# A four-stage convolution network on one core: order of the tap stages' work, of the first bias products, of the layer changes, and another form of the gates

## The chip, the cores and the metric

The kernel runs on one core of a Trainium2 chip. The metric is the time of one launch in microseconds of the device, the median over several runs. The engines are called PE (TensorE: matrix products), DVE (VectorE), ACT (ScalarE), POOL (GpSimd) and SP (SyncE, which only issues transfers here). Transfers are issued from the queues of SP, ACT and POOL.

## The reference

Input x has 4 images of 256 channels and 56 x 56 points, in float32. Four layers follow, each as x = x + F(groupnorm(x)), with groups of 8 channels:

```python
# layer 0: involution: a 7x7 kernel for each point and each of 16 groups
h = einsum('bchw,oc->bohw', x, reduce_w) + reduce_b          # 64 channels
kern = einsum('bchw,oc->bohw', h, span_w) + span_b           # 16 * 49 taps for each point
out = (kern.reshape(b, G, 1, K*K, Ho, Wo) * patches).sum(axis=3)
# layer 1: two 3x3 convolutions, each with batch norm; relu(x + h)
# layer 2: involution as layer 0, with batch norm and relu after the reduce and after the sum
# layer 3: gates from Fourier transforms
cf = sigmoid(fft2(x).real.mean((-2, -1)) @ W.T + b)          # one value for each channel
sf = fft2(x.mean(1, keepdims=True)).real.mean(1)             # one value for each point
out = x * cf[:, :, None, None] + x * sf[:, None]
```

## The kernel before

All layers run in one program: `involution_layer(0)`, `conv_layer`, `involution_layer(2)`; the gates of layer 3 run inside layer 2, one image later. Channels lie on the 128 partitions, in two blocks (cb), and a block of an image is a tile of 128 x 3136 (`new_block`, three buffers). Each engine's instructions stand in the order in which the program writes them (`in_order`), so a step's place in the text is its place in its engine's queue. An engine waits only for what its next instruction needs, so a queue may run ahead of the others.

An involution works by units: image b, block cb, eight units. For each image `bottleneck` first makes h, the reduced input, as the tile `hp`: products of `redn` (the reduce weights times the norm's scale) and x into PSUM, then evictions with the bias `hb`. For layer 0's first image `begin` does this, in an order written out by hand. Each unit then has two stages:

- Tap stage, `tap_matrices`: 32 steps n, each with six products (L580) into a pair of PSUM banks, and an eviction into `kt` with the bias `zb_sb`, by ACT in six instructions (L591) for every third n and by DVE in one (L598) for the others. There are four such pairs of banks, for everything in these layers. `hooks` is a dictionary of other steps which are put in after the eviction of step n: the group norm's six steps for the block before (`norm_steps`: aggregate, product, small sums, product, power on POOL, shift), the channel mean, the gate factors, loads.
- Column stage, `apply`: seven columns tx of eight points. For each, 56 products of `kt` and a window matrix `xw` (L622), a sum on ACT and DVE, and then `next_windows` and `next_strip`. A strip is the normed input of one column with its border (`strip_sb`, one buffer), transposed by seven products (L396), copied to `xw` by ACT (L408), and shifted within `xw` by four transfers (L414, L416). There are three buffers of `xw`, so windows are three columns ahead. `early` and `late` hold steps put in before and after a column.

`zb_sb` comes from `window_biases`: 24 small products (L255) and one copy. In layer 0 it stands in `begin` ahead of the first norm; for layer 2 it is made at the beginning of the convolutions and goes through DRAM (`zb2_dram`).

`conv_layer` computes each 3 x 3 convolution with transformed columns: `row_weights` makes the transformed weights u1 to u4 (L1218 to L1225), `phases` spreads the normed input into four phases on ACT (L1290), `transform` makes the six tiles v on DVE (L1298 to L1320), then follow products (L1411, L1382, L1493). A list `after` gives the steps put in after each group of products.

In layer 2, `channel_mean` and `gate_factors` make cf and sf of the image before; sf goes through DRAM and comes back to all partitions. Its weights `w3` are loaded by SP into a part of the image's own block that is no longer used (`dead`). `gate_chunk` is one of 14 gates of an image, with 8 rows of a block each: load of x (`gx`, three buffers), four operations on POOL, and a store. `next_load` and `next_gate` take the load and the rest of the next one. With xn = rstd * x + shift, it computes x * (1 + cf * rstd) + cf * shift + xn * sf. The last image is done by `last_gates` and its companions in another form.

Of the kernel before, what the change touches and what calls it, by code (L numbers as in the profile page):

```python
# [16 lines left out]
P = 128  # L17
# [54 lines left out]
def net_kernel(  # L72
# [59 lines left out]
    for i in range(2):  # L132
        nc.scalar.dma_start(rp[i * R : (i + 1) * R, :], rpar)
    mhalf = const.tile([P, NB], F32, name="mhalf")
# [89 lines left out]

    def mark():
        return len(nc.cur_bb.bb.instructions)
# [23 lines left out]
    def window_biases(zb_sb, bias, ps):  # L250

        bias_f = bias[:G, KK * KK : KK * KK + ZN]
        for p in range(TP):
# [7 lines left out]
            )  # L261
        nc.scalar.copy(
# [17 lines left out]
    def involution_layer(layer, xin, xout, red, span, sb, xs_of, ahead=None, pending=None):  # L280

        with ExitStack() as es:
# [12 lines left out]
            def warm(n, by):  # L295

                ps = one_bank()
                for _ in range(n):
                    nc.tensor.matmul(ps[:, :P], ident_sb, by, start=True, stop=True)
# [6 lines left out]
            if layer == 0:  # L306
# [3 lines left out]
                nc.scalar.copy(norm_sb[:, 3, B - 1, 1, :], mhalf)  # L310

            red_sb = wpool.tile([P, NB, 2, R], F32, name="red_sb")

            def load_red():
                for i in range(2):
                    eng = nc.gpsimd if layer == 0 else nc.scalar
                    eng.dma_start(red_sb[:, :, i], red.rearrange("(cb p) r -> p cb r", p=P))

            if layer == 2:
                load_red()  # L320
# [41 lines left out]
            def next_strip():  # L362
# [15 lines left out]
                if layer == 2:  # L378
# [42 lines left out]
            def bottleneck(b):  # L421
# [4 lines left out]
                rstd, shift = norms[layer][b]  # L426

                redn = work.tile([P, NB, 2, R], F32, name="redn", bufs=1)
                for ci in range(NB):
                    nc.vector.tensor_scalar_mul(redn[:, ci], red_sb[:, ci], rstd[:, ci : ci + 1])  # L430
# [55 lines left out]
            def begin():  # L486
# [4 lines left out]
                biases = bias_table(scratch[:, n:], sb, nc.gpsimd.dma_start, nc.scalar.copy)  # L491
# [3 lines left out]
                load_red()  # L495
# [6 lines left out]
                window_biases(zb_sb, scratch[:, n:], one_bank())  # L502
                folds = batch_norms()
                sums0, sums1 = sums(0, 0), sums(0, 1)
                redn = work.tile([P, NB, 2, R], F32, name="redn", bufs=1)
                rstd, shift = norms[0][0]
                steps(sums0, NCHUNK)
                norm = norm_of(0, 0, 0, sums_of[0, 0])
                steps(norm, 2)
                warm(4, ident_sb)  # L510
                steps(norm, 2)
                warm(8, ident_sb)
# [7 lines left out]


                pairs = [two_banks() for _ in range(4)]
                bank = pairs[3][:, 1, :]
# [34 lines left out]
                for j in range(NH):  # L558
                    products(j, 1)
                for j in range(NH):  # L560
# [3 lines left out]
                    for py in range(min(rows, TY)):  # L564
                        dst = hp[:, py, :, a0 : a0 + n, :]
                        nc.scalar.activation(dst, s[:, py, :, :n, :], AF.Identity, bias=hb)
                return folds
# [1154 lines left out]
```

## Time and profile before

The median of three runs is 1817.9 us (1817.29 to 1822.03). One more execution was recorded by the profiler: 1812.46 us, of which 1810.7 are the span from the first to the last instruction. All times below are places in that span.

| what | from the profile |
|---|---|
| profiled execution, its span | 1812.46 us, 1810.7 us |
| mean granted clock of PE | 0.979 |
| tap products L580 | 392.1 us busy, 6144 passes |
| column products L622 | 379.0 us busy, 12544 passes |
| convolution products L1493, L1411, L1382 | 385.0, 212.3 and 98.6 us busy |
| tap evictions on DVE, L598 | 336, 319.8 us busy |
| tap evictions on ACT, L591 | 1056 instructions, 306.9 us busy |
| gate operations on POOL | L789 and L794 31.7 us each, L795 49.0, L796 48.7, 42 of each |
| layer 0, convolutions, layer 2 | up to about 507 us, to 1243 us, to the end |

How to read it: a product in float32 shows as two passes. PE's busy time counts matmuls whose ends are modelled, so a busy PE is not one at its peak. The granted clock is 1.00 at full speed, and in places of low activity it is 0.50. The time of an idle engine costs nothing unless the engine is the one that all others wait for.

### The profile page before, as it was taken

What the parts mean: (1) busy time and instruction counts of PE and PEld (TensorE: products, weight loads), DVE (VectorE), ACT (ScalarE), POOL (GpSimd) and SP (SyncE); (2) the same over time, 40 slices, a digit from 0 to 9 for tenths busy, and PEclk for the clock granted to TensorE, in tenths of its full rate; (3) what the DMA queues carried; (4) which work ended last, traced back from release to release, by engine and by line L of the source; (5) the groups of instructions that cost most, each with busy time, mean ns of one, the idle gap of its engine ahead of it and who ended that gap; (6) DMA issues with size and microseconds to landing.
All of it is one profiled execution on the core that took longest, in us unless ns stands there. A gap on an engine that the chain in (4) does not pass through costs nothing.

```text
span 1810.7 us, 55835 instructions
## 1 busy us (share of the span) xinstructions
PE 1720.8 (95%) x24034; PEld 1514.9 (84%) x24034; DVE 1375.4 (76%) x2729; ACT 842.2 (47%) x1981; POOL 430.0 (24%) x626
## 2 busy tenths in 40 slices
PE   7999999999989999999999999997999999899988
PEld 6998989889878988998899889985988887887876
DVE  3787777776689988898889888875777677677775
ACT  3566556555532322322232222113767567577564
POOL 2333433245210000000000000000000374563572
PEclk9999999999989999999999999998999999999997
DMA  2545534454651201120121111031534566665653
GB/s 85 158 154 165 164 119 143 159 159 116 209 174 49 69 26 63 63 70 30 59 73 59 41 60 34 34 135 49 161 132 149 168 218 188 202 210 168 169 156 127
DMA packets 66004, 215.77 MB, mean 119 GB/s; under 512 B 13237, under 2 KB 20926, under 8 KB 62046
## 3 DMA queue, kind: packets, MB, share of 16 engines
q1 hardware_dynamic: 48718, 145.24, 25.7%
q0 software_dynamic: 14688, 64.78, 11.3%
q8 instruction: 190, 3.11, 0.7%
q10 hardware_dynamic: 2352, 2.18, 0.4%
q14 instruction: 56, 0.46, 0.1%
HBM read 76.30 MB, written 49.15 MB: 69 GB/s over the span
## 4 chain that ended last, share of the span: by engine, by line
PE 76%; DVE 9%; ACT 6%; DMA 4%; issue 2%; POOL 2%; SPq 1%; ACTq 0%; POOLq 0%; DVEq 0%
PE mm L1493 19%; PE ps L580 18%; PE ps L622 14%; PE mm L1411 10%; PE mm L1382 5%; PE ps L396 5%; DMA xw<-xw 4%; ACT kt L591 3%; PE ps L459 2%; DVE un L642 1%; DVE kt L598 1%; ACT xw L408 1%; ACT hp L478 1%; SPq L414 1%; DVE res L1486 1%
## 5 line engine op out<-in xcount | busy, mean ns | idle before, releaser
L580 PE MATMUL ps<-hp,z_sb 64*126 64x133 f32 x6144 | 392.1, 281 | 16.2 <-ACT kt L591 7.0
L622 PE MATMUL ps<-kt,xw 126*32 126x48 f32 (+1 forms) x12544 | 379.0, 236 | 24.1 <-DMA xw<-xw 12.1
L622 PEld LDWEIGHTS ps<-kt,xw 126*32 126x32 f32 (+1 forms) x12544 | 341.9, 122 | 68.2 <-issue 46.3
L580 PEld LDWEIGHTS ps<-hp,z_sb 64*126 64x126 f32 x6144 | 369.1, 187 | 34.6 <-ACT kt L591 12.7
L598 DVE TENSOR_TENSOR kt<-ps,zb_sb 126x798 f32<-126x798 f32 x336 | 319.8, 981 | 90.1 <-PE ps L580 89.5
L1493 PE MATMUL mm<-v,u_sb 128*128 128x280 f32 (+1 forms) x1728 | 385.0, 385 | 3.4 <-DVE v L1318 3.4
L1493 PEld LDWEIGHTS mm<-v,u_sb 128*128 128x128 f32 x1728 | 327.9, 190 | 57.5 <-DVE v L1318 3.8
L591 ACT ACTIVATE kt<-ps,zb_sb 126x133 f32<-126x133 f32 x1056 | 306.9, 442 | 96.2 <-PE ps L580 95.6
L1411 PE MATMUL mm<-v,u_sb 128*128 128x252 f32 (+1 forms) x936 | 212.3, 388 | 3.4 <-DVE v L1302 3.4
L1411 PEld LDWEIGHTS mm<-v,u_sb 128*128 128x128 f32 x936 | 178.3, 192 | 33.8 <-issue 3.5
L1530 POOL DMA_DIRECT2D x<-xs x24 | 13.1, 546 | 683.2 <-DVE xs L1529 427.4
L642 DVE SCALAR_TENSOR_TENSOR un<-ps,s,un 128x240 f32<-128x240 f32 x224 | 102.5, 457 | 85.7 <-ACT un L637 81.5
L642 DVE SCALAR_TENSOR_TENSOR un<-ps,par_sb,un 128x240 f32<-128x240 f32 x224 | 98.3, 457 | 87.1 <-ACT un L635 82.8
L1478 ACT ACTIVATE res<-xs,shift,norm_sb 128x1120 f32<-128x1120 f32 (+1 forms) x24 | 30.2, 1259 | 236.3 <-DVE xs L1529 107.3
L408 ACT COPY xw<-ps 126x896 f32<-126x896 f32 x112 | 101.4, 906 | 47.9 <-PE ps L396 37.7
L647 POOL TENSOR_TENSOR xs<-un,xs 128x240 f32<-128x240 f32 x112 | 72.3, 664 | 192.4 <-DVE un L642 192.3
L396 PE MATMUL ps<-ident_sb,strip_sb 128*126 128x128 f32 x784 | 111.7, 283 | 6.1 <-POOL strip_sb L381 5.8
L635 ACT ACTIVATE un<-ps,par_sb 128x240 f32<-128x240 f32 x112 | 50.1, 448 | 115.7 <-PE ps L622 113.4
L1382 PE MATMUL mm<-xs,u_sb 128*128 128x126 f32 (+1 forms) x792 | 98.6, 277 | 1.3 <-DVE xs L1345 0.9
L396 PEld LDWEIGHTS ps<-ident_sb,strip_sb 128*126 128x126 f32 x784 | 84.9, 142 | 17.0 <-POOL strip_sb L381 6.9
L637 ACT ACTIVATE un<-ps,bn_t,s 128x240 f32<-128x240 f32 x112 | 60.0, 538 | 83.3 <-PE ps L622 72.1
L1382 PEld LDWEIGHTS mm<-xs,u_sb 128*128 128x128 f32 x792 | 94.5, 191 | 2.4 <-issue 1.0
(254 smaller groups left out, 1925.8 us busy)
## 6 DMA issues: line engine op xcount, KB each, us to landing
xw<-xw SPq DMA_DIRECT2D x168, 252.0 KB
xw<-xw SPq DMA_DIRECT2D x224, 126.0 KB
xw<-xw POOLq DMA_DIRECT2D x56, 252.0 KB, 4.7
xs<-x SPq DMA_DIRECT2D x24, 560.0 KB
x<-xs POOLq DMA_DIRECT2D x8, 1568.0 KB, 8.2
xs<-x SPq DMA_DIRECT2D x8, 1568.0 KB
xs<-in_x_dram SPq DMA_DIRECT2D x6, 1568.0 KB
x<-xs SPq DMA_DIRECT2D x6, 1568.0 KB
```

The source lines that it names most:

```text
L396: nc.tensor.transpose(ps[:Q, k * P : (k + 1) * P], flat[:, k * Q : (k + 1) * Q], ident_sb)
L408: nc.scalar.copy(xw[:, :NSB, :], ps[:Q, : NSB * P].rearrange("q (n c) -> q n c", n=NSB))
L580: nc.tensor.matmul(ps[:Q, i, k * NT : (k + 1) * NT], z_sb[i * R : (i + 1) * R, cb * GB // 2 + gp, z0 : z0 + Q], hp[i * R : (i + 1) * R, py ...
L591: nc.scalar.activation(kt[:, g0 + i, pb, :, k], ps[:Q, i, k * NT : (k + 1) * NT], AF.Identity, bias=zb_sb[:, cb * GB + g0 + i, p0 + k : p0 ...
L598: nc.vector.tensor_tensor(kt[:, g0 : g0 + 2, pb], ps[:Q, :, : PB * NT].rearrange("q i (k t) -> q i t k", k=PB), zb_sb[:, cb * GB + g0 : cb ...
L622: nc.tensor.matmul(v[m * j : m * j + m, i, :, k * TP : (k + 1) * TP], xw[:, window(ty), m * j : m * j + m], kt[:, ng * j : ng * j + ng, :, ...
L637: nc.scalar.activation(part, o[0], AF.Identity, bias=bn["t4"][:, cb : cb + 1], scale=bn["s4"][ng][:, 0, cb : cb + 1])
L642: nc.vector.scalar_tensor_tensor(part, o[e], s, part, ALU.mult, ALU.add)
L647: nc.gpsimd.tensor_tensor(dst, u, dst, ALU.add)
L1382: nc.tensor.matmul(ps[:, co * m : (co + 1) * m], u[ci][:, co * P : (co + 1) * P], v2[:, e, : n // 2, ci * WT : (ci + 1) * WT], start=(ci = ...
L1411: nc.tensor.matmul(ps, u1_sb[:, ci, dy, k, co * P : (co + 1) * P], v[:, k, dy * NB + ci : (dy + n - 1) * NB + ci + 1 : NB, :], start=(j == 0),
L1493: nc.tensor.matmul(ps, u2_sb[:, ci, dy, k, co * P : (co + 1) * P], v[:, k, dy * NB + ci : (dy + n - 1) * NB + ci + 1 : NB, :], start=(j == 0),
```

## The change

- `red_sb`, the reduce weights, becomes one constant tile for both involutions; `redn` becomes a constant too. Layer 2's weights are loaded in `begin_conv` (near the end of layer 0) by SP instead of at layer 2's beginning by ACT's queue, and `redn` of its first image is made in `begin_last`, by `norm_weights`, in the last but one convolution.
- In `begin` the bias's load goes from POOL's queue to ACT's. Of the 24 bias products 14 stay ahead of the first norm and 10 go behind the reduce products; the copy follows the evictions into `hp`. The PSUM pairs are taken earlier, and the first norms and the warming products use one of them.
- An activation at the beginning is a Sigmoid instead of a copy (its result is overwritten later).
- Tap stages: ACT evicts n = 2, 5, ... 29 (10) instead of 0, 3, ... 30 (11).
- Layer 2's start: the first two strips are made by POOL; the first strip stands ahead of `bottleneck(0)`, and two windows stand ahead of the tap products instead of between them.
- In units 1 and 2 of layer 2 the steps of the norm stand at other n. `gate_factors` begins at n = 8 instead of 17, and w3 is loaded into the buffers of `sfb` (all images but the last).
- Gates: xn * (sf + cf + 1/rstd) - shift/rstd. Loads of sf are steps of their own, two ahead, and loads and gates stand at other places.
- Convolutions: in `row_weights` the third operation of both blocks follows the first two of both; at the beginning three products of 448 columns follow the bias products, and the weights' third operations follow the third step of `transform`.

```diff
+    red_sb = const.tile([P, NB, 2, R], F32, name="red_sb")
+    def load_red(red, eng):
+        for i in range(2):
+            eng.dma_start(red_sb[:, :, i], red.rearrange("(cb p) r -> p cb r", p=P))
+    def norm_weights(layer, b):
+        redn = redn_of[layer, b] = new_redn()
+        for ci in range(NB):
+            nc.vector.tensor_scalar_mul(redn[:, ci], red_sb[:, ci], norms[layer][b][0][:, ci : ci + 1])
...
-                nc.scalar.copy(norm_sb[:, 3, B - 1, 1, :], mhalf)
+                nc.scalar.activation(norm_sb[:, 3, B - 1, 1, :], mhalf, AF.Sigmoid)
...
-                if layer == 2:
+                if layer == 2 and len(strips) > 2:
                     nc.scalar.activation(dst, img, AF.Identity, bias=shift, scale=rstd)
                 else:
                     nc.gpsimd.tensor_scalar(dst, img, rstd, shift, ALU.mult, ALU.add)
...
-                biases = bias_table(scratch[:, n:], sb, nc.gpsimd.dma_start, nc.scalar.copy)
+                biases = bias_table(scratch[:, n:], sb, nc.scalar.dma_start, nc.scalar.copy)
...
-                window_biases(zb_sb, scratch[:, n:], one_bank())
+                pairs = [two_banks() for _ in range(4)]
+                bank = pairs[3][:, 1, :]
+                biases = window_biases(zb_sb, scratch[:, n:], bank[:, R:])
+                steps(biases, 14)
...
                 for j in range(NH):
                     products(j, 1)
+                steps(biases, TP - 14)
...
                         nc.scalar.activation(dst, s[:, py, :, :n, :], AF.Identity, bias=hb)
+                run(biases)
                 return folds
...
-                    if n % 3 == 0:
+                    if n % 3 == 2:
...
-                w3_sb = [dead(b, 1, 4 * CR * W + ci * C, C) for ci in range(NB)]
+                w3_sb = [new_sf()[:, :C] if b < B - 1 else dead(b, 1, 4 * CR * W + ci * C, C) for ci in range(NB)]
...
-                nc.vector.tensor_mul(scale, cf, norms[3][b][0])
-                nc.vector.tensor_scalar_add(scale, scale, 1.0)
-                nc.vector.tensor_mul(bias, cf, norms[3][b][1])
+                nc.vector.reciprocal(back, rstd)
+                nc.vector.tensor_add(cfx, cf, back)
+                nc.vector.scalar_tensor_tensor(back, shift, -1.0, back, ALU.mult, ALU.mult)
...
+            def load_sf(b, j):
+                sf_of[b, j] = new_sf()
+                nc.gpsimd.dma_start(sf_of[b, j], sf_dram[b][j : j + 1].to_broadcast([P, CR * W]))
...
-                nc.gpsimd.tensor_scalar(xs, xs, scale, bias, ALU.mult, ALU.add)
-                nc.gpsimd.tensor_tensor(xn, xn, sf, ALU.mult)
-                nc.gpsimd.tensor_tensor(xs, xs, xn, ALU.add)
+                nc.gpsimd.tensor_scalar(xs, sf_of[b, j], 1.0, cfx, ALU.mult, ALU.add)
+                nc.gpsimd.tensor_tensor(xs, xs, xn, ALU.mult)
+                nc.gpsimd.tensor_scalar(xs, xs, 1.0, back, ALU.mult, ALU.add)
+                if cb == 1 and j + 2 < NCHUNK:
+                    load_sf(b, j + 2)
...
+                next_strip()
                 run(bottleneck(0))
                 hooks0[3] = list(pending[0])
-            next_strip()
-            for i in range(NXW):
-                hooks0.setdefault(2 + 5 * i, []).extend((next_windows, next_strip))
+                for _ in range(NXW - 1):
+                    next_windows()
+                    next_strip()
+                hooks0[7] = [next_windows, next_strip]
...
-                        place(hooks, g, (19, 20, 22, 23, 25, 26))
+                        place(hooks, g, (15, 19, 20, 24, 25, 26))
...
-                            place(hooks, gate_factors(pb), (17, 24, 27, 28, 30, 31))
+                            place(hooks, gate_factors(pb), (8, 24, 27, 28, 30, 31))
+                            chunks.extend(gate_chunk(pb, j, c) for j in range(NCHUNK) for c in range(NB))
+                            for n in (20,):
+                                hooks.setdefault(n, []).append(next_load)
...
-                        for n in (16, 22, 28):
-                            hooks.setdefault(n, []).extend((next_gate, next_load))
+                        for n in (14, 18, 22, 26):
+                            hooks.setdefault(n, []).extend((next_load, next_gate))
...
                     if cb == 0:
-                        chunks.extend(gate_chunk(b - 1, j, c) for j in range(NCHUNK) for c in range(NB))
-                        late[1] += [next_load, next_load]
-                    for tx in range(2, NTX) if cb == 0 else range(NTX - 1):
-                        late[tx] += [next_gate, next_load]
+                        late[0] += [lambda b=b, j=j: load_sf(b - 1, j) for j in range(2)]
+                    for tx in range(1, 6) if cb == 0 else range(NTX - 2):
+                        late[tx] += [next_load, next_gate]
...
         raw_weights(1, 0, 1, nc.sync)
+        load_red(red2, nc.sync)
...
                     tt(u2, w0, w2, ALU.add)
                     tt(u1, u2, w1, ALU.add)
+                    yield
+                for w0, w1, w2, u1, u2, u3, u4 in ws:
                     tt(u2, u2, w1, ALU.subtract)
-                    yield
+                yield
...
+            ps = one_bank()[:, : CR * W]
+            for _ in range(3):
+                nc.tensor.matmul(ps, ident_sb, room["rows"][:, : CR * W], start=True, stop=True)
             load_rows(1, xin)
             g = input1(0)
-            for _ in range(4):
+            for _ in range(3):
                 next(g)
+            next(weights1)
+            next(g)
             run(weights1)
...
             load_block(blocks[0, cb], src[2][0][cb])
+        norm_weights(2, 0)
```

## The prediction

> **What bounds the kernel now.** I read the page's busy shares, then the windows by stage (span cut at tap stages and layer changes), then TensorE's timeline for what ended each gap, then the other engines there.
>
> From the page:
> ```profile
> PE 1720.8 (95%) x24034; PEld 1514.9 (84%) x24034; DVE 1375.4 (76%) x2729; ACT 842.2 (47%) x1981; POOL 430.0 (24%) x626
> ```
> TensorE is the bound; all that can be won is its 90 us of idleness, plus what it runs at half clock. The windows (us, then busy of PE, PEld, DVE, ACT, POOL, granted clock, DMA share, GB/s) say where that lies:
> ```profile
> 0.00:38.60 38.60, 28.11 (x113) 21.77 (x113) 12.09 (x38) 11.66 (x40) 11.75 (x25) 1.00 0.32 100
> 159.33:213.30 53.97, 53.21 (x1224) 49.56 (x1223) 39.97 (x72) 31.72 (x87) 20.48 (x30) 1.00 0.50 157
> 900.00:1235.00 335.00, 334.85 (x1763) 295.76 (x1762) 283.63 (x591) 75.61 (x126) 9.97 (x17) 1.00 0.17 61
> 1235.00:1264.00 29.00, 17.92 (x92) 11.43 (x91) 12.68 (x29) 10.74 (x27) 1.67 (x6) 0.78 0.20 55
> 1384.20:1452.00 67.80, 61.36 (x1268) 54.31 (x1269) 47.43 (x99) 41.79 (x100) 21.57 (x28) 0.97 0.55 165
> 1648.50:1719.00 70.50, 65.01 (x1317) 57.91 (x1317) 50.46 (x97) 44.60 (x109) 26.19 (x36) 0.95 0.53 150
> ```
> Layer 0's units and the middle of the convolutions have nothing to give (0.8 us idle in 54, 0.15 in 335). The start, the two layer changes and layer 2's units (3 to 7 us idle each) have. TensorE's timeline names the gaps (last bracket: idle before, releaser):
> ```profile
> 17.61 0.59 PE L207 MATMUL ps<-mv,gavg_sb 128*128 128x1 f32 x2
> 38.60 3.75 PE L580 MATMUL ps<-hp,z_sb 64*126 64x133 f32 x36 [2.15 <-ACT hp L566]
> 517.93 37.19 PE L1411 MATMUL mm<-v,u_sb 128*128 128x280 f32 x144 [3.37 <-DVE v L1302]
> 1247.04 0.99 PE L437 MATMUL ps<-norm_sb,red_sb 128*128 128x1 f32 x4 [6.81 <-DMA red_sb<-in_red_dram]
> 1259.64 4.36 PE L580 MATMUL ps<-hp,z_sb 64*126 64x133 f32 x36 [4.27 <-ACT hp L478]
> 1338.33 0.35 PE L207 MATMUL ps<-mv,gavg_sb 128*128 128x1 f32 x2 [0.94 <-DVE mv L204]
> 1342.07 0.35 PE L218 MATMUL ps<-d,gavg_sb 128*128 128x1 f32 x2 [1.14 <-DVE d L215]
> 1411.43 4.09 PE L580 MATMUL ps<-hp,z_sb 64*126 64x133 f32 x36 [0.86 <-ACT kt L591]
> 1569.35 4.43 PE L622 MATMUL ps<-kt,xw 126*64 126x96 f32 x104 [3.77 <-DMA xw<-xw]
> 1672.93 1.05 PE L732 MATMUL ps<-first,xs 128*128 128x1 f32 x8 [1.85 <-ACT kt L591]
> 1673.91 3.98 PE L580 MATMUL ps<-hp,z_sb 64*126 64x133 f32 x36
> ```
> 36 tap products take 2.3 us at full clock (1338.61), so the 3.98, 4.09 and 4.36 above are half-clock stretches after a gap. The wait at 1672.93 is put down to ACT, but w3's transfer was issued at 1669.62 to 1670.45, and in the image before the same product waited for w3 openly (0.52 and 0.41 at 1540.6 and 1541.4): I read it as w3.
>
> **What the Trainium skill says.** "TensorE: Matmul & The Clock Gate", section "HAM oscillation — how this bites in real kernels": idle gaps over about 3.4 us halve the clock. The trace agrees: after the stop at 1240.2 the windows from 1246 to 1250 show clock 0.50, and 510 to 522 as well. "SBUF — State Buffer", section "Who interferes with whom": a DVE operation with two SBUF inputs and a GpSimd one that reads SBUF block each other. Agrees: DVE's L649 takes 0.41 us alone (1318.18) and 1.22 beside POOL's L796 (1648.78). "ScalarE: Activation LUTs", section "What ACT_TABLE_LOAD costs": 1283 ns and a drain of about 1380 ns. The load at 1411.39 took 1.28 us; of a drain nothing is seen, it began 0.02 us after ACT's last work.
>
> **The change part by part**, against the profiled execution's 1812.46 us (span 1810.7).
>
> *Start.* mv of the first norm is ready at 10.7 us, but its product comes at 17.61, behind 24 bias products (48 passes, 10.42 us from 7.26). 14 stay ahead: 10 x 0.434 = 4.3 us earlier. The bias load moves from POOL to ACT's queue, behind the table load and its activation (4.39): on POOL it landed 5.4 us after issue, at 6.9; on ACT, unseen here, I bound it by landing from 6.5 (2 us) to 8.5, so the norm gains 2.7 to 4.3. Everything up to hp shifts with it (hp evictions end at 38.5 now). The 10 products put behind the last reduce products take 3.1 us (0.155 a pass at 507) to 4.3, where TensorE idles 2.15 now. Taps begin at 35.2 to 37.7 instead of 38.6. zb's copy (1.1 us on ACT) now stands behind the hp evictions and ahead of the first eviction of taps, which loses about 0.4. Taken: -2.0 (-3.5 to +0.5).
>
> *Into the convolutions.* Two of six weight operations (0.98 us each) go behind v1's, but v4 also waits for ACT's eight phases, which end at 514.73: v4 can start 0.6 us sooner, no more. Three products of 448 columns fill 514.6 onwards; at half clock about 4.5 us (estimate: twice the 0.375 a pass that 0.42 for 504 columns at L529 gives, six passes), so L1411 begins near 519 instead of 517.9, but at full clock, where 4.1 us ran at half. -1.0 (-2 to +1.5). The step that weights2 gains is covered by the convolution's slots.
>
> *Into layer 2.* red_sb becomes a constant, loaded by SP in layer 0's last tap stage (two issues of some 0.4 us, SP idle there); redn is made in the last but one convolution (2 x 0.24 us of DVE, TensorE-bound stage). Then L437 and the reduce products need not wait for the transfer (issued 1243.13). What is late next: hb, whose DVE operation stands behind L1529 (ends 1244.4), two shifts and a memset that follows POOL's memset (1244.16): about 1245.0. The hp evictions (20, 8.34 us) then run 1245.0 to 1253.4 instead of 1251.47 to 1259.8: -6.4. If the PSUM of the convolution is let go only at 1243.04 like its SBUF, the first pair is done near 1246.7: -4.8. The first two strips go to POOL (about 1.0 us each, idle there) and 14 transposes stand before the taps, under the hp evictions: 2 x 0.98 us leave the tap stage; the two xw copies (0.91 each) follow hp on ACT, which DVE's first two evictions cover. The clock is half again (TensorE mostly waits for 6 us), so that stays. -8.5 (-10.5 to -5).
>
> *Hooks of units 1 and 2.* mv's product gets four groups after its aggregate instead of one, as layer 0 has it without a wait: 2 x (0.94 + 1.14) = 4.2. Taken -4.0 (-4.5 to -1.5).
>
> *w3 and the table.* w3 goes to sfb buffers and is issued before the m stores, not after. It waits for POOL's last gate of the image before (1520.4 now; SP gets there at 1521.5); behind it on SP are the m stores, at 1535: 14 us of slack. Gone: 0.93, and 1.85 with the half clock after it (3.98 - 2.35 = 1.6). The Sigmoid table is loaded at the start instead of the Copy one, so the load of 1.28 us at 1411.39 goes, with part of 0.86 + 1.7 there. 4.4 + 2.6 = 7.0 seen, -5.5 taken (-8 to -3), as some of it overlaps the hooks' gain.
>
> *ACT takes n = 2, 5 ... 29.* One eviction per unit, 16 in all, goes from ACT (6 x 0.29 us) to DVE (0.95). DVE has 22 x 0.95 = 21 us and 2 to 4 of norms in a stage of 25 to 29. At a boundary both engines come free together (1319.81): groups 0 and 1 now both wait for DVE, group 3 behind the column sums and the aggregate, so the 0.64 <- ACT goes and two waits of 0.2 to 0.4 come. At the end group 31 sets kt as before. +0.5 (-3 to +5, 16 units at -0.2 to +0.3).
>
> *Gates.* Per gate a tensor_tensor (1.16 us) becomes a tensor_scalar (0.755): POOL's period falls from about 5.85 to 5.45, 42 times, none on the path. POOL runs ahead of its hooks, held by gx, sf and the norms' pow. Its 14 gates end before the boundary (now 1520.4 against 1516.5), which frees DVE's two-input operations there: about -1. The factors stay three small DVE operations; sf's first two loads go in front of POOL's gates (0.55 each), which wait for sf anyway. Against it: one gx stands loaded ahead instead of two, and gate 0 starts as sf lands. DMA is the limit beside the column products: xw moves 756 KB a column in 4.1 us (189 GB/s) and a gate some 573 KB in 5.45, at a measured ceiling of 230 to 260 GB/s; waits for xw in layer 2 sum to about 10 us. A gate moves from the second to the first unit's columns, gx 0 leaves them, x's load (1410.60, behind w3's product) goes 5 us earlier, out of the way. +0.5, so -0.5 in all (-6 to +6).
>
> Sum: -2.0 -1.0 -8.5 -4.0 -5.5 +0.5 -0.5 = -21.0: 1791.5 against 1812.46. The warm products' and first norms' new PSUM pair waits for nobody. The median of the runs stands 5.4 above the profiled execution; carried over, 1817.9 - 21 = 1797.
>
> **Rivals.** *More goes (1787):* the xw waits shrink by 6 and the half-clock stretches after them too; for it, x's earlier load; against it, the traffic is the same. *Half is given back (1808):* hb is held longer at 1245 (4 us less) and columns wait 6 us more for xw. *No change (1817):* the first part of layer 2 waits for something not seen now, with waits for xw on top. *Slower (1827):* DVE becomes the bound of the tap stages. Place: groups 0 to 8, where DVE takes two groups behind its columns' backlog; for it, DVE at 0.95 of 1.1 us a group that it has, POOL's interference (L694 1.35 us instead of 0.38 at 1597); against it, layer 0's slack above. From 1.4 us a unit (16 x 1.4 = 22) it eats all; 1827 needs 1.9.
>
> **How the numbers follow.** Forecast, 1790 to 1804: 0.60. More: 0.15. Half: 0.12. No change: 0.06. Slower: 0.07. A change of 0.3% (5.5 us) is about what can be told from none. Faster 0.87, same 0.06, slower 0.07. The parts' ends add up to -37 and +3.5, seldom all together; the range is 1785 to 1808.
>
> **What would show it.** Right: no wait for red_sb, taps of layer 2 beginning 12 to 14 us after the last convolution product instead of 19.4; L207 at 13 to 15 us; no wait over 0.3 at mv and d in units 1 and 2; one table load; no wait at w3's product. Wrong: tap stages of layer 0 over 25.5 us, waits for xw over 12 us in sum, or hp evictions of layer 2 that start more than 8 us after the last convolution product.

## The result, and the profile after

The changed kernel takes 1797.18 us in the median of four runs (1793.2 to 1799.56), the one before, run beside it, 1819.18 (1817.29 to 1822.03): a ratio of 0.9877, 95% interval 0.9852 to 0.9902. That is the predicted time, but not by the predicted sum: one part went the wrong way and another gave more.

First the page's busy times of the changed kernel (engine, us, share of the span, instructions):
```profile
PE 1716.7 (96%) x24040; PEld 1507.5 (84%) x24040; DVE 1385.3 (77%) x2745; ACT 813.5 (45%) x1882; POOL 406.2 (23%) x627
```
TensorE is busy for 4 us less with nearly the same products (six passes more), and the mean granted clock is 0.985 instead of 0.979; the rest of the span's 19.3 us (1810.7 to 1791.4) is idleness. ACT has 29 us less and DVE 10 more, mostly by the tap order. The windows over the stretches that answer to those shown of before (us; busy of PE, PEld, DVE, ACT, POOL; granted clock; DMA share; GB/s):
```profile
0.00:44.32 44.32, 29.23 (x112) 21.16 (x113) 12.10 (x38) 10.58 (x40) 11.28 (x24) 0.96 0.28 87
166.00:220.00 54.00, 53.02 (x1222) 49.30 (x1221) 40.84 (x73) 30.02 (x81) 20.48 (x30) 1.00 0.50 156
900.00:1235.00 335.00, 334.85 (x1764) 295.39 (x1763) 287.78 (x599) 75.36 (x125) 9.96 (x17) 1.00 0.17 61
1239.00:1268.00 29.00, 24.58 (x202) 18.54 (x201) 18.32 (x38) 15.81 (x37) 3.87 (x8) 0.88 0.33 105
1378.50:1442.90 64.40, 59.50 (x1268) 52.49 (x1267) 47.59 (x100) 38.98 (x92) 25.00 (x36) 1.00 0.63 191
1635.00:1705.50 70.50, 66.02 (x1382) 59.00 (x1383) 54.74 (x104) 44.56 (x108) 24.68 (x36) 1.00 0.59 171
```
Layer 0's unit and the convolutions are as before. At the entry to layer 2 TensorE is busy for 24.6 of 29 us instead of 17.9; unit 2 of layer 2 takes 64.4 us instead of 67.8, at clock 1.00 instead of 0.97. But the start, up to the first tap product, takes 44.32 us instead of 38.60.

Cut by the starts of the tap and column stages in TensorE's timeline (first product `hp,z_sb`, first product `kt,xw`), units of layer 2 counted from 0, the whole span adds up:

| stretch (us) | before | after | difference | predicted |
|---|---|---|---|---|
| start, to the first tap product | 38.6 | 44.3 | +5.7 | -2.0 |
| layer 0, to its last column stage | 437.0 | 437.7 | +0.7 | in the tap order's +0.5 |
| last column stage and convolutions, to their last product | 764.6 | 762.3 | -2.3 | -1.0 |
| last convolution product to layer 2's first column stage | 49.4 | 40.6 | -8.8 | -8.5 |
| tap stages of units 1 to 7 of layer 2 | 223.4 | 203.3 | -20.1 | -10.0 with the next row |
| column stages of units 0 to 6 | 232.8 | 237.3 | +4.5 | |
| last column stage and end | 64.8 | 65.8 | +1.0 | 0 |

TensorE's timeline of the changed kernel names what stands at each place (start, busy, instruction; last bracket: idle before, releaser):
```profile
11.12 6.15 PE L273 MATMUL ps<-ident_sb,xs 16*126 16x16 f32 x28 [11.12 <-ACT xs L265]
17.20 0.58 PE L217 MATMUL ps<-mv,gavg_sb 128*128 128x1 f32 x2
...
20.53 0.59 PE L228 MATMUL ps<-d,gavg_sb 128*128 128x1 f32 x2 [0.83 <-DVE d L225]
...
26.30 3.65 PE L540 MATMUL ps<-xs,redn 128*128 128x504 f32 x8 [1.57 <-DVE redn L531]
...
34.29 7.24 PE L540 MATMUL ps<-xs,redn 128*128 128x504 f32 x14 [0.39 <-DVE hb L568]
41.46 2.37 PE L273 MATMUL ps<-ident_sb,xs 16*126 16x16 f32 x20
44.32 3.12 PE L593 MATMUL ps<-hp,z_sb 64*126 64x133 f32 x36 [0.49 <-ACT hp L578]
...
526.51 34.34 PE L1441 MATMUL mm<-v,u_sb 128*128 128x280 f32 x144
...
1244.94 0.58 PE L447 MATMUL ps<-norm_sb,red_sb 128*128 128x1 f32 x4 [0.63 <-DVE xs L1554]
...
1257.19 7.54 PE L593 MATMUL ps<-hp,z_sb 64*126 64x133 f32 x96 [1.24 <-ACT hp L488]
...
1333.38 0.38 PE L217 MATMUL ps<-mv,gavg_sb 128*128 128x1 f32 x2
1337.38 0.38 PE L228 MATMUL ps<-d,gavg_sb 128*128 128x1 f32 x2
...
1656.67 1.05 PE L748 MATMUL ps<-first,sfb 128*128 128x1 f32 x8
1657.84 2.32 PE L593 MATMUL ps<-hp,z_sb 64*126 64x133 f32 x36
```
(L217, L228, L273, L447, L540, L593, L748, L1441 were L207, L218, L255, L437, L529, L580, L732, L1411.) The waits for `red_sb`, for mv and d in unit 1, and for w3 are gone; the 36 tap products after w3's take 2.32 us, full clock, instead of 3.98. The last convolution product ends at 1244.3, so the taps begin 12.9 us after it instead of 19.4. At the start, the first bias product comes 3.9 us later than before (11.12 against 7.26); L217 is nevertheless 0.4 us earlier; but from L217 to the taps it is 27.1 us instead of 21.0.

### The profile page after: what moved, and what is told of

Read it like the earlier page. It is cut to its first block, busy times and chain, and to the rows that moved or that the text cites. A ratio compares the mean times of both kernels' runs of the same rounds, so it can differ in the third digit from the quotient of the medians.

```text
span 1791.4 us, 55774 instructions
## 1 busy us (share of the span) xinstructions
PE 1716.7 (96%) x24040; PEld 1507.5 (84%) x24040; DVE 1385.3 (77%) x2745; ACT 813.5 (45%) x1882; POOL 406.2 (23%) x627
## 4 chain that ended last, share of the span: by engine, by line
PE 68%; DVE 19%; ACT 4%; DMA 4%; issue 3%; POOL 2%; SPq 1%; POOLq 0%; ACTq 0%; DVEq 0%
PE mm L1523 17%; PE ps L593 14%; PE ps L635 14%; PE mm L1441 9%; DVE kt L611 6%; PE mm L1412 5%; PE ps L406 3%; DMA xw<-xw 3%; DVE un L655 3%; PE ps L469 1%; DVE res L1516 1%; DVE xs L1375 1%; DVE st L1105 1%; ACT kt L604 1%; ACT hp L488 1%
## 5 line engine op out<-in xcount | busy, mean ns | idle before, releaser
L635 PE MATMUL ps<-kt,xw 126*32 126x48 f32 (+1 forms) x12544 | 381.8, 235 | 27.8 <-issue 12.2
L593 PE MATMUL ps<-hp,z_sb 64*126 64x133 f32 x6144 | 383.2, 279 | 8.4 <-DVE kt L611 4.6
L593 PEld LDWEIGHTS ps<-hp,z_sb 64*126 64x126 f32 x6144 | 363.6, 185 | 24.4 <-DVE kt L611 6.8
L611 DVE TENSOR_TENSOR kt<-ps,zb_sb 126x798 f32<-126x798 f32 x352 | 332.9, 980 | 60.4 <-PE ps L593 49.2
L604 ACT ACTIVATE kt<-ps,zb_sb 126x133 f32<-126x133 f32 x960 | 280.1, 441 | 107.3 <-PE ps L593 107.3
L1441 PE MATMUL mm<-v,u_sb 128*128 128x252 f32 (+1 forms) x936 | 209.5, 384 | 0.0
L1441 PEld LDWEIGHTS mm<-v,u_sb 128*128 128x128 f32 x936 | 176.4, 189 | 30.5 <-issue 0.8
```

The lines of the kernel that those rows point to most:

```text
L593: nc.tensor.matmul(ps[:Q, i, k * NT : (k + 1) * NT], z_sb[i * R : (i + 1) * R, cb * GB // 2 + gp, z0 : z0 + Q], hp[i * R : (i + 1) * R, py ...
L604: nc.scalar.activation(kt[:, g0 + i, pb, :, k], ps[:Q, i, k * NT : (k + 1) * NT], AF.Identity, bias=zb_sb[:, cb * GB + g0 + i, p0 + k : p0 ...
L611: nc.vector.tensor_tensor(kt[:, g0 : g0 + 2, pb], ps[:Q, :, : PB * NT].rearrange("q i (k t) -> q i t k", k=PB), zb_sb[:, cb * GB + g0 : cb ...
L635: nc.tensor.matmul(v[m * j : m * j + m, i, :, k * TP : (k + 1) * TP], xw[:, window(ty), m * j : m * j + m], kt[:, ng * j : ng * j + ng, :, ...
L1441: nc.tensor.matmul(ps, u1_sb[:, ci, dy, k, co * P : (co + 1) * P], v[:, k, dy * NB + ci : (dy + n - 1) * NB + ci + 1 : NB, :], start=(j == 0),
```

## The start: two causes

DVE's timeline there, changed kernel:
```profile
19.73 0.16 DVE L220 COPY gm<-ps 128x1 f32<-128x1 f32 x1 [8.32 <-PE ps L319]
...
24.77 0.16 DVE L148 TENSOR_SCALAR norm_sb<-ps 128x1 f32<-128x1 f32 x1 [4.30 <-PE ps L319]
```
The copy of `gm` reads what L217 wrote, yet it is released by L319, the warming products that follow L217. They write the other bank of the same PSUM pair, `pairs[3]`; before the change they had a pair of their own, and the copy was released by L207. L319 ends at about 19.7, L217 at 17.8: the norm waits for products that serve only to keep TensorE busy, and again at 24.77. ACT's row says how late the bias was, asked for at 4.69 on its queue:
```profile
4.69 0.35 ACTq L262 DMA_DIRECT2D xs<-in_sb_dram  x1
10.83 0.23 ACT L265 COPY xs<-xs 16x49 f32<-16x49 f32 x1 [6.44 <-DMA xs<-in_sb_dram]
```
Two edits tell the causes apart, alone and together (all experiments are edits of the changed kernel):
```diff
s_pool, s_both:
-                biases = bias_table(scratch[:, n:], sb, nc.scalar.dma_start, nc.scalar.copy)
+                biases = bias_table(scratch[:, n:], sb, nc.gpsimd.dma_start, nc.scalar.copy)
s_warm, s_both:
-                warm(4, ident_sb, pairs[3][:, 0, :])
+                warm(4, ident_sb, pairs[2][:, 0, :])
...
-                warm(8, ident_sb, pairs[3][:, 0, :])
+                warm(8, ident_sb, pairs[2][:, 0, :])
```


> The changed kernel with the start's bias load back on POOL's queue. Theory 'landing': the start lost time because the bias landed at 10.75 us; then the bias products begin near 7.3 instead of 11.12 us, L217 comes at 13.4 to 14 instead of 17.20, and the taps begin near 40.5 instead of 44.32; the kernel gains 3 to 4 us. Theory 'shared pair' (the first norm's small sums wait for the warming products, which write the other bank of the same pair): the distance from L217 to the reduce products L540 stays at 9.1 us here.

> The changed kernel with the two groups of warming products in another PSUM pair than the first norm's sums. Theory 'shared pair': the copy of gm on DVE (L220) comes 0.6 us after L217 instead of 2.5, the next sum right after L228, and the distance from L217 to L540 falls from 9.1 us to the 5.4 of the kernel before; taps begin near 40.6 instead of 44.32. Theory 'landing' alone: L217 stays at 17.2 and the distance stays near 9 us, because the products themselves are slow there.

> Both edits of the start together. If the two losses are separate they add up: L217 at 13.4 to 14, L540 5.4 us later, taps at 36.5 to 37.5 instead of 44.32, some 7 us less than the changed kernel in time (near 1790 us). If one covers the other, taps begin at 40 or later.

DVE's timeline of s_warm shows the right releasers again:
```profile
17.57 0.16 DVE L220 COPY gm<-ps 128x1 f32<-128x1 f32 x1 [6.27 <-PE ps L217]
...
19.70 0.16 DVE L148 TENSOR_SCALAR norm_sb<-ps 128x1 f32<-128x1 f32 x1 [1.40 <-PE ps L228]
```
TensorE's timeline of s_both:
```profile
6.96 6.15 PE L273 MATMUL ps<-ident_sb,xs 16*126 16x16 f32 x28 [6.96 <-ACT xs L265]
13.04 0.59 PE L217 MATMUL ps<-mv,gavg_sb 128*128 128x1 f32 x2
...
18.61 3.55 PE L540 MATMUL ps<-xs,redn 128*128 128x504 f32 x8
...
26.50 5.54 PE L540 MATMUL ps<-xs,redn 128*128 128x504 f32 x14 [0.39 <-DVE hb L568]
31.98 2.37 PE L273 MATMUL ps<-ident_sb,xs 16*126 16x16 f32 x20
34.83 3.98 PE L593 MATMUL ps<-hp,z_sb 64*126 64x133 f32 x36 [0.49 <-ACT hp L578]
```

| | L217 | L217 to L540 | first taps | time (us) |
|---|---|---|---|---|
| before | 17.61 | 5.4 | 38.60 | 1819.18 beside the changed kernel, 1814.67 beside the three below |
| changed | 17.20 | 9.1 | 44.32 | 1797.18 |
| s_pool | 13.08 | 8.9 | 40.04 | 1797.01, one run |
| s_warm | 16.95 | 6.0 | 39.17 | 1788.61, one run |
| s_both | 13.04 | 5.6 | 34.83 | 1784.53, ratio to before 0.9818 (0.9793 to 0.9843) |

Both theories hold, and the losses are separate: 4.3 us for the queue of the load and 5.2 us for the shared pair, 9.5 together. In s_warm 1.7 of the 5.2 us come from the last 14 reduce products, which take 5.54 us, about as before (5.55), and not 7.24; this part is a matter of the clock (see the end). The interval of s_both lies below the changed kernel's. (The total of s_pool shows nothing of its 4.3 us: its entry into the convolutions took 1.7 us longer than the changed kernel's and its column stages in layer 2 3.3 us longer, in text that is the same. Single runs are read by their stages.)

## Layer 2's units: one part undone at a time

```diff
taps0:
-                    if n % 3 == 2:
+                    if n % 3 == 0:
hooks_old:
-                        place(hooks, g, (15, 19, 20, 24, 25, 26))
+                        place(hooks, g, (19, 20, 22, 23, 25, 26))
w3_old:
-                nc.scalar.activation(norm_sb[:, 3, B - 1, 1, :], mhalf, AF.Sigmoid)
+                nc.scalar.copy(norm_sb[:, 3, B - 1, 1, :], mhalf)
...
-                w3_sb = [new_sf()[:, :C] if b < B - 1 else dead(b, 1, 4 * CR * W + ci * C, C) for ci in range(NB)]
+                w3_sb = [dead(b, 1, 4 * CR * W + ci * C, C) for ci in range(NB)]
...
-                            place(hooks, gate_factors(pb), (8, 24, 27, 28, 30, 31))
+                            place(hooks, gate_factors(pb), (17, 24, 27, 28, 30, 31))
gates_form and gates_all (gates_all also has the old places and loads of gates and sf):
-                nc.gpsimd.tensor_scalar(xs, sf_of[b, j], 1.0, cfx, ALU.mult, ALU.add)
-                nc.gpsimd.tensor_tensor(xs, xs, xn, ALU.mult)
-                nc.gpsimd.tensor_scalar(xs, xs, 1.0, back, ALU.mult, ALU.add)
+                nc.gpsimd.tensor_scalar(xs, xs, scale, bias, ALU.mult, ALU.add)
+                nc.gpsimd.tensor_tensor(xn, xn, sf_of[b, j], ALU.mult)
+                nc.gpsimd.tensor_tensor(xs, xs, xn, ALU.add)
nostore:
-                nc.gpsimd.dma_start(ov[b, cb][:, at], xs)
```


> The changed kernel with only the tap order undone (ACT evicts n = 0, 3, ... 30 again). My prediction's theory: the order is worth about nothing, +0.5 us (-3 to +5); layer 0's tap stages go back from 24.8 and 26.6 to 24.8 and 26.2 us, and layer 2's tap stages stay within 0.5 us each. Rival 'order': the order itself is what shortened layer 2's tap stages beyond what the hooks and w3 explain (units 3, 4 and 7: 2.0 to 3.3 us each); then those go back by 1 to 2 us each and the kernel is 5 to 10 us slower.

> The changed kernel with the norm's steps of units 1 and 2 of layer 2 back at n = 19, 20, 22, 23, 25, 26. My prediction's theory: each of the two tap stages (28.6 and 31.1 us now) waits again for mv and d, about 0.94 and 1.14 us, so each goes to 30.2 to 31 and 32.7 to 33.5 us, 4 us in all. Rival 'gates': those waits came from DVE's queue and not from the distance of the steps; then they stay under 0.3 us each here.

> The changed kernel with w3 back in the dead part of the block and asked for at n = 17, and with a copy instead of the Sigmoid at the start, so that the table is loaded in layer 2 again. My prediction's theory: the tap stages of units 2, 4 and 6 (31.1, 30.7 and 30.0 us now) lengthen by 2.9 (table), 0.9 and 3.5 us (w3 and the half clock after it), 5.5 to 7 in sum. Rival: the waits were transfers' and gates' luck; then the three stages lengthen by less than 3 us in sum.

> The changed kernel with the old four operations of a gate (two of them with two inputs) and the old factors, at the new places. Theory 'form' (the operation with two inputs on POOL delays DVE's evictions in the tap stages): the tap stages of units 3, 5 and 7 (27.0, 28.2, 27.7 us now, 29.1, 28.7, 31.0 before the change) go back up by 1 to 3 us each, and the waits for DVE's kt with them. Theory 'place': they stay within 0.5 us, POOL's time for a gate grows from about 5.45 to 5.85 us and nobody waits for it.

> The changed kernel with the gates' old operations and also their old places and loads (loads of sf one ahead, gates at n = 16, 22, 28 and up to the sixth column). Theory 'form': the tap stages of units 3, 5 and 7 lengthen as in the run with the form alone. Theory 'place': here alone they go back to about 29.1, 28.7 and 31.0 us, since the last gates of an image then run into the next tap stage. My prediction's sum had the gates at -0.5 us (-6 to +6) in all, so a total within 6 us of the changed kernel's either way.

> The changed kernel without the gates' stores to the output for the first three images (42 stores of 229 KB are left out). Theory 'transfers' (the column stages of layer 2 give back 4.7 us because the windows' transfers share the DMA engines with the gates): the column stages of units 2, 4 and 6, 33.3, 33.9 and 32.8 us now, fall towards layer 0's 29.3 to 30.5, 5 to 10 us in sum. Rival 'issue': the shifts of the windows start late because of what their queue does before them; then the stages shorten by less than 3 us in sum.

What came out (us, by stage starts; columns: the seven column stages of units 0 to 6 together):

| kernel | tap 1 | 2 | 3 | 4 | 5 | 6 | 7 | taps 1-7 | columns 0-6 |
|---|---|---|---|---|---|---|---|---|---|
| before | 31.8 | 36.1 | 29.1 | 32.7 | 28.7 | 34.1 | 31.0 | 223.4 | 232.8 |
| changed | 28.6 | 31.1 | 27.0 | 30.7 | 28.2 | 30.0 | 27.7 | 203.3 | 237.3 |
| s_both | 28.6 | 31.1 | 27.9 | 30.4 | 27.1 | 30.4 | 27.8 | 203.2 | 236.2 |
| hooks_old | 31.1 | 33.4 | 28.1 | 30.1 | 27.8 | 30.6 | 27.9 | 209.0 | 238.9 |
| w3_old | 28.0 | 33.5 | 27.5 | 33.3 | 27.8 | 34.2 | 27.9 | 212.3 | 235.0 |
| gates_form | 28.6 | 31.1 | 27.0 | 31.2 | 28.6 | 30.9 | 27.7 | 205.1 | 243.8 |
| gates_all | 28.5 | 31.1 | 29.7 | 30.7 | 29.1 | 30.9 | 29.1 | 209.0 | 241.6 |
| nostore | 28.3 | 31.1 | 28.3 | 30.0 | 27.9 | 30.0 | 28.2 | 203.8 | 237.7 |
| taps0 | 29.5 | 32.0 | 28.2 | 30.7 | 28.2 | 30.7 | 28.9 | 208.1 | 231.1 |

The seven kernels whose steps in these tap stages are the same, nostore's stores apart (changed, s_pool, s_warm, s_both, nostore, entry_red, nowarm_conv), show how far a stage repeats: stages 1 and 2 to 0.4 us, the others to between 0.8 and 1.4, the sum of the seven from 202.5 to 204.6. Their column stages lie between 236.2 and 240.7. The single totals of hooks_old, w3_old, both gates kernels and nostore, 1795.8 to 1804.5 us, settle nothing by themselves.

*Hooks.* Stages 1 and 2 go back by 2.5 and 2.3 us, 4.8 in all, and TensorE's timeline of hooks_old shows the waits again (unit 1):
```profile
1336.63 0.35 PE L217 MATMUL ps<-mv,gavg_sb 128*128 128x1 f32 x2 [1.15 <-DVE mv L214]
...
1340.59 0.35 PE L228 MATMUL ps<-d,gavg_sb 128*128 128x1 f32 x2 [1.36 <-DVE d L225]
```
My theory holds; the rival falls.

*w3 and the table.* Stages 2, 4 and 6 go back by 2.5, 2.6 and 4.2 us: 9.3, more than the 5.5 that I took and the 7 expected at most. TensorE waits 0.97, 0.95 and 2.23 us there, and after each of these waits a stretch at half clock follows: the next 36 tap products take 3.27 us in unit 2 and 3.56 in unit 4 instead of 2.3. In unit 4 of the kernel before, a wait of 0.93 had been followed by 2.32 us, full clock, so that cost was in no term. TensorE's timeline of w3_old, units 2 and 6:
```profile
1402.98 3.27 PE L593 MATMUL ps<-hp,z_sb 64*126 64x133 f32 x36 [0.97 <-ACT cf L755]
...
1661.67 0.35 PE L748 MATMUL ps<-first,xs 128*128 128x1 f32 x2 [1.70 <-DMA xs<-in_w_dram]
1662.55 0.83 PE L748 MATMUL ps<-first,xs 128*128 128x1 f32 x6 [0.53 <-DMA xs<-in_w_dram]
```
In unit 6 the wait of 1.85 that the profile of before put down to ACT is here openly a wait for w3's transfer, 1.70 and 0.53. That reading is confirmed. In unit 2 it is a wait for cf, which stands behind ACT's table load (one load in the whole changed kernel, two in the kernel before and in w3_old):
```profile
1401.37 1.28 ACT L755 ACT_TABLE_LOAD   x1
```

*Gates.* With the old form alone, stages 3, 5 and 7 change by 0.0, +0.4 and 0.0 us: theory 'form' falls. With the old places and loads too they go back to 29.7, 29.1 and 29.1 (+4.9 together, and 3.4 more than the longest of the seven kernels). So theory 'place' holds by its numbers for units 3 and 5, for less than half of unit 7's 3.2 us, and not by its reason. In the column stages, which neither theory named, gates_form has 243.8 us, the most of all, and gates_all 241.6, both past the 240.7 of the seven kernels: the new form may be worth a few us there. One profile of each doesn't show it. The timelines of gates_all in unit 3, first DVE, then POOL, then TensorE:
```profile
1458.99 1.72 DVE L707 TENSOR_SCALAR mean<-cmean,norm_sb 128x32 f32<-128x32 f32 x2
```
```profile
1457.48 0.56 POOL L149 TENSOR_TENSOR norm_sb<-norm_sb,mhalf 128x1 f32<-128x1 f32 x1 [10.14 <-DVE norm_sb L148]
1458.05 0.71 POOL L807 TENSOR_SCALAR gn<-gx,norm_sb 128x448 f32<-128x448 f32 x1
...
1459.54 1.13 POOL L813 TENSOR_TENSOR gn<-gn,sfb 128x448 f32<-128x448 f32 x1
```
```profile
1460.86 0.24 PE L715 MATMUL ps<-one,mean 128*32 128x1 f32 x8 [0.89 <-DVE mean L707]
1461.66 1.70 PE L718 MATMUL ps<-xs,mean 128*32 128x448 f32 x14 [0.56 <-DVE kt L611]
```
A gate's operation with two inputs (L813) stands beside DVE's two small operations of the channel mean (L707, put in at n = 13), which take 1.72 us together, and TensorE waits 0.89 us for them and 0.56 for the eviction behind. Units 5 and 7 show the same two waits. POOL's timeline of the changed kernel there:
```profile
1454.56 0.56 POOL L149 TENSOR_TENSOR norm_sb<-norm_sb,mhalf 128x1 f32<-128x1 f32 x1 [11.05 <-DVE norm_sb L148]
1455.08 0.58 POOL L803 DMA_DIRECT2D gx<-x  x1
...
1457.26 1.15 POOL L812 TENSOR_TENSOR gx<-gx,gn 128x448 f32<-128x448 f32 x1
```
In both kernels POOL goes on at once behind the norm's power (L149, at n = 12), so n = 14 or 16 makes no difference to it here. What differs is the order of the pair: the changed kernel issues the next load first (0.58 us) and then does the gate, and its two-input operation (L812) begins after the channel mean, whose two operations take 0.81 us there, from 1455.67 on. This is read from the timelines. The order of load and gate was not tried alone, nor were the new operations at the old places.

*Tap order.* taps0 takes 1791.08 us, ratio to before 0.986 (0.9829 to 0.989), not to be told from the changed kernel. By stages, the new order takes 4.8 us off the tap stages (203.3 against 208.1) and the column stages are longer by 6.2. The kernel below that also has the old order has 208.3 and 233.5, and before had 232.8; the eleven kernels with the new order have 235 to 244. So what came back in the column stages, +4.5, goes with the tap order, as far as three profiles against eleven show it. How the order reaches the columns is open: in units 3 and 5 TensorE is idle for 3.0 us together in the changed kernel and for 0.9 in taps0, but for 3.0 in the kernel before too, which has the old order.

*Stores.* Without 42 stores the column stages take 237.7 us instead of 237.3, and those of units 2, 4 and 6 are 34.1, 34.0 and 33.9 us, not 29 to 30. The windows of unit 2's column stage, changed kernel and nostore:
```profile
1409.50:1442.90 33.40, 29.54 (x830) 25.85 (x828) 21.79 (x50) 18.17 (x26) 23.31 (x33) 1.00 0.79 224
```
```profile
1408.10:1442.20 34.10, 29.53 (x830) 25.96 (x828) 23.07 (x51) 18.18 (x26) 20.81 (x29) 0.99 0.74 196
```
The DMA engines are less busy, and TensorE waits as long. That the gates' stores delay the windows is refuted; the loads were not taken away. The rival's number came, but its reason is not seen either: in the column stages of units 2, 4 and 6 of the changed kernel SP issues the first shift 0.02 to 0.07 us after ACT's copy (once 0.62). What is long is the issuing itself. The last of the four shifts is issued 3.3 to 4.7 us after the copy, in layer 0's units of the same block 2.5 to 3.5; there the program gives one of the four to POOL's queue, in layer 2 all four to SP's. What that is worth was not tried.

## The layer changes, and the best version

```diff
entry_red:
-        load_red(red2, nc.sync)
...
-        norm_weights(2, 0)
...
+            if layer == 2:
+                load_red(red, nc.scalar)
             z_sb = wpool.tile([P, G // 2, ZN], F32, name="z_sb")
nowarm_conv:
-            ps = one_bank()[:, : CR * W]
-            for _ in range(3):
-                nc.tensor.matmul(ps, ident_sb, room["rows"][:, : CR * W], start=True, stop=True)
best (with both edits of the start and the tap order of taps0):
-                steps(biases, 14)
+                steps(biases, 8)
...
-                steps(biases, TP - 14)
+                steps(biases, TP - 8)
```


> The changed kernel with the reduce weights loaded by ACT's queue at the beginning of layer 2 again, and redn made there. My prediction's theory: the constant is worth 4.8 to 6.4 of the 8.8 us that layer 2's start gained; L447 waits for the transfer again, and the taps begin about 18 us after the last convolution product instead of 12.9, the column stage about 46 instead of 40.6. Rival: the strips and windows ahead of the taps gave most of it; then the taps begin less than 3 us later than now.

> The changed kernel without the three products of 448 columns at the start of the convolutions. My prediction's theory: the first products L1441 then begin up to 4 us earlier but run at half clock, and the norm's product L217 comes 47 to 48 us after the first bias product instead of 46.7: within 1.5 us of now. Rival 1: the warm products are worth 3 us or more. Rival 2: they only cost, and L217 comes 2 us or more earlier without them.

> The changed kernel with four edits: bias load on POOL's queue, warming products in another pair, 8 instead of 14 bias products ahead of the first norm, and the old tap order (n = 0, 3, ... 30). From the runs before: the first two give taps at 34.8 instead of 44.3 us. With 8 bias products, L217 should come at 10.7 to 11 instead of 13.04 us, and the taps at 33 to 34.5, as the late bias products grow from 2.4 to 3.8 us, beside the evictions into hp. The tap order gave the same total or 2 to 3 us less. Expected time 1779 to 1785 us; rival: the colder TensorE makes the reduce products slower (7.2 instead of 5.5 us for the last 14 passes), and taps begin at 35.5 or later.

*Entry to layer 2.* TensorE in entry_red (last convolution product ends at 1247.2):
```profile
1247.84 0.58 PE L449 MATMUL ps<-norm_sb,red_sb 128*128 128x1 f32 x4 [0.63 <-DVE xs L1555]
1252.38 7.62 PE L471 MATMUL ps<-xs,redn 128*64 128x504 f32 x28 [3.97 <-DVE redn L241]
...
1264.17 6.04 PE L595 MATMUL ps<-hp,z_sb 64*126 64x133 f32 x96 [1.20 <-ACT hp L490]
```
The edit did not bring the old wait for the transfer back: L449 waits 0.63 us for DVE, as now. `red_sb` stays a constant tile, so its load need not wait until the convolutions' buffers are let go. What the run shows is the other half: `redn`, made on DVE behind the last operations of the convolution, comes 4.0 us too late. Taps begin 17.0 us after the last convolution product (12.9 now), column stages 43.0 (40.6 now). So making `redn` early is worth 4.1 us at the taps and 2.4 at the columns. Neither theory is hit in full. The old wait was not tried alone, nor were the strips and windows ahead of the taps, so how the other 6.4 of the 8.8 us divide is open.

*Into the convolutions.* In nowarm_conv L1441 begins 10.0 us after the first bias product (12.5 with the warming products, 10.8 before), and runs at half clock for its first 5.7 us:
```profile
523.17 37.02 PE L1441 MATMUL mm<-v,u_sb 128*128 128x280 f32 x144 [1.47 <-DVE v L1332]
560.03 0.28 PE L217 MATMUL mm<-mv,gavg_sb 128*128 128x1 f32 x2
```
L217 comes 46.85 us after the first bias product, against 46.68 with them and 47.83 in the kernel before. The three products buy the full clock at about the price of their own time. Without them 1.0 of the 1.1 us that this entry gained is still there. But the gain itself is not clear of the spread: with the same text at this place L217 comes after 46.6 to 46.7 us in most runs, after 48.3 in s_pool and hooks_old, where the half clock lasts 13.65 us instead of 10.24, and after 46.1 in s_both, where it lasts 6.83. Of before there is one profile. The order of the weights' operations, the other edit that moves work here, was not tried alone.

*Best.* 1782.41 us in the median of five (1780.65 to 1785.22), ratio to before 0.9812 (0.9784 to 0.9839): below the changed kernel, not to be told from s_both. Fewer bias products ahead of the norm bought nothing. L217 came at 11.04, but TensorE's timeline has the rival's slow products:
```profile
24.00 7.24 PE L540 MATMUL ps<-xs,redn 128*128 128x504 f32 x14 [0.39 <-DVE hb L568]
31.17 3.69 PE L273 MATMUL ps<-ident_sb,xs 16*126 16x16 f32 x32
35.35 3.98 PE L593 MATMUL ps<-hp,z_sb 64*126 64x133 f32 x36 [0.49 <-ACT hp L578]
```
Taps at 35.35 instead of 34.83.

## Why the prediction was right, and where it was wrong

The time was right to the microsecond by luck: two errors cancelled, and the runs of one kernel lie 5 to 6 us apart. The start was off by +7.7 us (+5.7 against -2.0), layer 2's units by -5.6 (-15.6 against the -10.0 of hooks, w3 and gates).

- *Start, wrong in sign.* Two steps failed. The bias load on ACT's queue was bounded by landing at 6.5 to 8.5 us; it was there at 10.8, which costs 4.3 us against POOL's queue (s_pool). The one landing of this load that the profile showed, 5.4 us after its issue, would have put it at 9.8; the bound took 2 to 4 us instead, without a reason. And "the warm products' and first norms' new PSUM pair waits for nobody" was said without following who reads the pair: DVE's sums do, and waited for the warming products (s_warm, 5.2 us). "Everything up to hp shifts with it" failed for the same reason. With both mended the taps begin at 34.8, 3.8 us earlier than before, just ahead of the 35.2 to 37.7 that I gave.
- *Into the convolutions, right by its number* (-1.1 at L217 against -1.0), which the spread of this place doesn't tell from nothing. Of the two means named, the weights' order fits (L1441 0.8 us earlier in nowarm_conv than before, 0.6 named); the warming products give nothing net.
- *Into layer 2, right.* The wait for `red_sb` is gone, and one of the three means has its share measured (redn, 2.4 us). The hp evictions were put 4.8 us after the last convolution product (1245.0 against 1240.2); they start 4.7 after it (ACT at 1249.01). Taps came 12.9 us after it, within the 12 to 14 given, column stages 8.8 us earlier against 8.5.
- *Hooks, right in mechanism, a little too small:* -4.8 against -4.0, just past the range's end of -4.5.
- *w3 and the table, right in mechanism, too small:* -9.3, below the range's end of -8. The 7.0 that the profile showed was cut to 5.5 "as some of it overlaps the hooks' gain"; no such loss was seen. Stages 4 and 6 lost 6.8 us where waits and half clock of 4.4 were counted; the half clock after unit 4's wait (3.56 us for 36 products instead of 2.32) was not among them.
- *Gates, right to doubt, wrong size:* the -0.5 (-6 to +6) were -5.7 in the tap stages (gates_all), with perhaps more in the column stages. I looked for the gain at the unit's boundary and in the operations; the timelines show it beside the channel mean, where a load's issue now stands ahead of the gate. And "DMA is the limit beside the column products" is not borne out: with 196 instead of 224 GB/s (nostore) the columns take as long.
- *Tap order, right as a sum:* nothing, but as -4.8 in the tap stages and about as much back in the column stages, where the +0.5 had neither. The rival that DVE becomes the bound did not come: layer 0's tap stages after the first are 24.8 and 26.6 us against 24.8 and 26.2. The longer kind was over the 25.5 that I named as a sign of failure before the change already: the sign was badly set. Another sign was waits for xw over 12 us: by name they are 8.9 us in layer 2 (10.6 before), but 7.4 us more of the idleness in the column stages has no releaser in the trace (1.9 before), so it decides little.
- *The clock, read wrongly in part.* The stop at 1240.2 fits the rule quoted in the prediction. The other place, 510 to 522, does not: in the kernel before the half clock begins at 510.33, while TensorE runs the small bias products without a gap from 507.13 to 514.56. And half clock followed waits of 0.86 us (1411.43, before) and 0.95 us (1531.88, w3_old). Here the measurement decides: a long idle gap is not needed.

The tap stages' sums of hooks_old, w3_old, gates_all and taps0 lie 5.7, 9.0, 5.7 and 4.8 us above the changed kernel's, 25.2 together, and 20.1 were gained. They may overlap in part; with single profiles and a spread of 2.1 us in each sum this is not shown.

## What to carry to other kernels

When buffers are merged or shared, ask for every reader what the last writer ahead of it will now be: products that nobody reads can hold up a chain through the other half of a tile. A transfer at the start is priced by its queue and its place in it, and a load that others wait for is left where its landing has been seen. When a total comes out as predicted, cut it by stages before believing the sum.

## Not expected of the hardware

- The same 14 reduce products in the same order took 5.54 us in s_warm and s_both and 7.24 in best, in the changed kernel and in every other edit of it; the changed kernel's granted clock was 0.76 over them, one stretch at half clock. In entry_red, whose start has the changed kernel's text, the eight reduce products before them took 5.71 us instead of 3.65 too. s_both and best differ ahead of these products only by six bias products. What decides it is open.
- Late bias products took 0.12 us a pass (2.37 for 20), early ones 0.22 (6.15 for 28). The trace's record of the clock begins only at 25.19 us in the changed kernel, so the 1.00 of the view says nothing of the early ones; L217 right behind them took 0.58 us and at 29.79 us 0.28. Half clock at the start would fit both; it is not shown.
- A load of 16 short rows asked for at 4.69 us on ACT's queue was usable at 10.83, beside x's loads (DMA share 0.85 in the first 10 us).
